# Turning a later batch's x over beside the first layer's projections, and the first batch's statistics from PSUM

## The chip, the cores and the metric

The kernel runs on one core of a Trainium2 chip. The metric is device time in microseconds of one execution. Times come from separate executions; the profile is of one more execution, recorded by the hardware profiler.

## The reference, cut to what matters

The input x has 8 batches of 32 x 32 positions with 512 channels, in fp32; N = 1024 positions. Two layers follow each other, and each adds an attention to its input:

```python
x = x + L0(_gn(x))   # 16 heads of 32: softmax(q k^T / sqrt(32)) v, then w_proj and b_proj
x = x + L1(_gn(x))   # 4 heads of 128, with relative position logits, then Wo
def _gn(v):          # 32 groups of 16 channels: mean and variance over positions and channels
    g = v.reshape(B, H, W, 32, 16)
    return (g - mean(g)) / sqrt(var(g) + 1e-5)
```

In each layer q, k and v are products of the normalised x (1024 x 512) with a 512 x 512 matrix each. Batches don't depend on each other.

## The kernel before

**Layout.** x comes as rows of channels, and the kernel wants it with channels on the partitions. Batch 0 is turned over by TensorE (`load_first`, L1163). The others are loaded in pieces by `load_blocks` (L289): four DMAs of 64 KB bring one half of one chunk of 128 channels, in blocks of 32 x 32, into a buffer with the tag "row", and a VectorE transpose of 128x512 turns the blocks over. The tag has three buffers, and the output (`put_out`, L1358) uses the same three: its transpose writes one, and four DMAs empty it.

**Statistics.** `look_at` (L304) runs bn_stats on each half (512 elements) of a chunk and, after the second, bn_aggr. `group_norm` (L320) averages over groups of 16 channels by two small transposes and six small VectorE instructions, has GpSimd raise the variance to the power -1/2 (rstd, L357), and normalises in four `tensor_scalar` instructions (L361). With `apart=True` the averaging and the normalising lie in different stages.

**Products.** Each 512 x 512 projection is made of two units, and each unit of seven products in place of eight (Strassen's scheme, Winograd's form). Four sums of quarters of x are made by VectorE (`forming`, L403); sums of quarters of the weights are made once and kept in DRAM. `seven` (L467) runs a unit over three PSUM banks, x, y and z. In order: product 0 into x, ACT copies it to p1; product 5 into y, and VectorE adds a = y + p1 (L481); product 1 into x; product 4 into y, and b = y + p1 (L489); product 6 into z, ACT copies it to p7; product 2 into y, addition c12; product 3 into z, addition c21 (L646); and c22 on GpSimd (L650). It yields after each product, so that other work can be woven in.

**The order of the work.** The kernel is written as generators. `side_by_side` (L1409) runs the first layer's attention of batch b (`attention_0`, 64 steps, each of 8 score matmuls, an exponential on ACT, 4 matmuls into acc, and an addition of 128x2048 on VectorE, L823) beside a list of other work, `rest`, in proportion to given costs. For a batch b in the middle, `rest` holds, in this order:

1. `after_0` and `after_1`: output projections of the first layer of batch b-1 and of the second layer of batch b-2 (with `put_out`);
2. `second`: the second layer's q, k and v of batch b-1, and its position logits;
3. `attention_1`: the second layer's attention of batch b-1, with `load` of batch b+1 woven in (`load_apart`, L1148, fetches the turned x from DRAM, normalises and forms sums);
4. `before_0`: the first layer's q, k and v of batch b+1.

`woven(main, side, start, gap, places)` (L1397) takes one piece of `side` wherever main's step count, less `start`, is in `places` modulo `gap`. Around this, a scheduler places each instruction in its engine's order; `tc.issue_after(...)` holds an instruction behind another in that order. [...] The weights are loaded by `Stream` (L199), seven products ahead.

**turn_ahead** (L1128) turns batch b+1 over ahead of `load_apart`, for b = 1 to 6. In each of eight steps it starts the load of the next half, transposes the present one (L1139), takes its statistics, and stores the turned half to DRAM (L1141). It ends with the averaging and rstd. It is woven around items 1 and 2 at every sixth step from the third:

```python
            if coming is not None:
                rest = [woven(chain(*rest), later(turn_ahead, b + 1, coming), 3, 6)]
```

Where this stands in the code, `rest` holds items 1 and 2; `attention_1` and `before_0` are appended later.

**load_first.** TensorE transposes batch 0 into eight PSUM banks: four of a wide tile for the first half of the positions, four others for the second. ACT copies each bank to SBUF (L1189). Then TensorE runs six matmuls with no use for their result, into the wide tile ("idle", L1193), VectorE takes the statistics of the copies chunk by chunk, and the copies are normalised and summed (`forms`). `before_first` starts with v's product 0.

Of the kernel before, what the change touches and what calls it, by code (L numbers as in the profile page):

```python
# [17 lines left out]
P = 128  # L18
# [9 lines left out]
def quick_path(  # L28
# [66 lines left out]
    def chunks(block):  # L95
        return [block[:, i, :] for i in range(CC)]
# [202 lines left out]
    def statistics(st, xT, cc, name):  # L299

        for h in range(NH):
            look_at(st, xT[cc][:, h * NB : (h + 1) * NB], cc, h, name)

    def look_at(st, half, cc, h, name):  # L304

        if "mv" not in st:
            st["mv"] = mvs[0]
            mvs.reverse()
        if h == 0:
            st["st"] = small.tile([P, NH, 6], F32, tag=f"st{name[0]}", name=f"st_{name}_{cc}", bufs=1)  # L310
        s = st["st"]
        nc.vector.bn_stats(s[:, h, :], half)
        if h < NH - 1:
            return
        nc.vector.bn_aggr(
            st["mv"][:, : 2 * CC].rearrange("p (s c) -> p c s", c=CC)[:, cc, :],
            s.rearrange("p h s -> p (h s)"),
        )

    def group_norm(st, xT, name, after=None, behind=None, out=None, apart=False):  # L320

        mv = st.pop("mv")

        def averages(out, src, tag):
            total = small.tile([P, 2], F32, tag=f"total{tag}", name=f"total{tag}_{name}")
            nc.vector.tensor_reduce(
                total, src.rearrange("p (g k) -> p g k", k=GROUP_CHANNELS), axis=AX.X, op=ALU.add
            )
            nc.vector.tensor_scalar(
                out.rearrange("p (g k) -> p g k", k=GROUP_CHANNELS),  # L330
                total.unsqueeze(2).to_broadcast([P, 2, GROUP_CHANNELS]),
                1.0 / GROUP_CHANNELS,
                None,
                op0=ALU.mult,
            )

        turned = small.tile([P, 32], F32, tag="turned", name=f"turned_{name}")

        with tc.issue_after(after().ins) if after is not None else nullcontext():
            nc.vector.transpose(turned, mv)  # L340
        avg = small.tile([P, 2, 32], F32, tag="avg", name=f"avg_{name}")
        averages(avg[:, 0, :], turned, 0)

        nc.vector.tensor_sub(turned, turned, avg[:, 0, :])
        nc.vector.tensor_mul(turned, turned, turned)
        averages(avg[:, 1, :], turned, 1)
        back = small.tile([P, 2, 32], F32, tag="back", name=f"back_{name}")
        nc.vector.transpose(back.rearrange("p a c -> p (a c)"), avg.rearrange("p a c -> p (a c)"))
        mean = back[:, 0, :CC]
        var = small.tile([P, CC], F32, tag="var", name=f"var_{name}")  # L350
        nc.vector.scalar_tensor_tensor(
            var, back[:, 0, CC : 2 * CC], GN_EPS, back[:, 1, :CC], op0=ALU.add, op1=ALU.add
        )
        if apart:
            yield 0
        rstd = small.tile([P, CC], F32, tag="rstd", name=f"rstd_{name}")
        nc.gpsimd.tensor_tensor(rstd, var, neg_half, op=ALU.pow)  # L357
        yield 0
        for cc in range(CC):
            with tc.issue_after(behind().ins) if behind is not None else nullcontext():  # L360
                nc.vector.tensor_scalar(  # L361
                    xT[cc] if out is None else out[cc],
                    xT[cc],
                    mean[:, cc : cc + 1],
                    rstd[:, cc : cc + 1],
                    op0=ALU.subtract,
                    op1=ALU.mult,
                )
            if cc % 2 or apart:
                yield 0  # L370
# [5 lines left out]
    begun = [None]  # L376
    half_done = [None]

    reader = [None]
    summed = [None]  # L380
    beside_norm = [False]

# [84 lines left out]
    def seven(fs, u, rows, sink, name, hook=None):  # L467

        product = taken(fs, u, rows)
        x = bank(f"x_{name}")
        product(x, 0, True)
        p1 = snapshot("e1", f"p1_{name}")
        nc.scalar.copy(p1, x)
        yield HC
        y = bank(f"y_{name}")
        product(y, 5, True)
        a = snapshot("es1", f"a_{name}")  # L480
        reader[0] = begun[0] = nc.vector.tensor_add(a, y, p1)  # L481
        sink.early(p1, a)
        yield HC
        product(x, 1, False)
        sink.c11(x)
        yield HC
        product(y, 4, False)
        b = snapshot("es1", f"b_{name}")
        reader[0] = half_done[0] = nc.vector.tensor_add(b, y, p1)  # L489
        sink.middle(b)  # L490
        yield HC
        z = bank(f"z_{name}")
        product(z, 6, True)
        p7 = snapshot("e1", f"p7_{name}")
        nc.scalar.copy(p7, z)  # L495
        yield HC
        product(y, 2, False)
        sink.c12(y, p1)
        if hook is not None:
            hook()  # L500
        yield HC
        product(z, 3, False)
        sink.c21(z, a)
        sink.c22(b, p7)
        yield HC

# [120 lines left out]
    class Plain:  # L627
# [15 lines left out]
            nc.vector.tensor_add(self.dst[1][0], self.shape(y), self.shape(p1))  # L643

        def c21(self, z, a):
            nc.vector.tensor_add(self.dst[0][1], self.shape(z), self.shape(a))  # L646

        def c22(self, b, p7):
            s = self.shape
# [478 lines left out]
    def turn_ahead(b, st):  # L1128

        parts = [(cc, h) for cc in range(CC) for h in range(NH)]  # L1130
        ahead = [load_blocks(b, *parts[0])]
        st["kept"] = [
            dram.tile([P, N], F32, tag="kept", name=f"d_0_{b}_{cc}", bufs=4 * CC) for cc in range(CC)
        ]
        for i, (cc, h) in enumerate(parts):
            if i + 1 < len(parts):
                ahead.append(load_blocks(b, *parts[i + 1]))
            t = mem.tile([P, NB], F32, tag="row", name=f"xt_{b}_{cc}_{h}", bufs=3)
            nc.vector.transpose(t, ahead.pop(0))  # L1139
            look_at(st, t, cc, h, f"0_{b}")  # L1140
            nc.sync.dma_start(st["kept"][cc][:, h * NB : (h + 1) * NB], t)  # L1141
            yield 0
        st["x0"] = []
        st["norm0"] = group_norm(st, st["x0"], f"0_{b}", behind=lambda: added[0], apart=True)
        for _ in range(2):
            yield next(st["norm0"])
# [16 lines left out]
    def load_first(st):  # L1163

        rows = block("x_rows", [P, NT, C])
        for t in range(NT):
            queue = nc.scalar if t % 2 else nc.sync
            queue.dma_start(rows[:, t, :], xf[0, t * P : (t + 1) * P, :])
        for m in (WV0, WQ0, WK0):
            m.fetch(nc.sync)  # L1170
        x = block("x0T_0")
        xT = chunks(x)
        for h in range(NH):
            if h == 0:
                whole = wide_tile("turned_0")
                banks = [whole[:, cc, :] for cc in range(CC)]
            else:
                banks = [bank(f"turned_1_{cc}") for cc in range(CC - 1)]
                banks.append(psum.tile([P, NB], F32, tag="acc", name="turned_1", bufs=1))
            for t in range(NT // NH):  # L1180
                for cc in range(CC):
                    nc.tensor.transpose(
                        banks[cc][:, t * P : (t + 1) * P],
                        rows[:, h * (NT // NH) + t, cc * P : (cc + 1) * P],
                        ident,
                    )
            for cc in (0, 2, 1, 3):
                part = xT[cc][:, h * NB : (h + 1) * NB]
                nc.scalar.copy(part, banks[cc])  # L1189

        idle = wide_tile("idle")
        for t in range(6):
            nc.tensor.matmul(idle[:, t % CC, :], ident, rows[:, t, :], start=True, stop=True)  # L1193
        for cc in (0, 2, 1, 3):
            statistics(st, xT, cc, "0_0")
        st["kept"] = put_away(xT, "0_0")

        xn = block("xn0_0")
        run(group_norm(st, xT, "0_0", out=chunks(xn)))
        st["xn"] = forms(xn, "xn0_0")  # L1200

# [293 lines left out]
    for b in range(B + 1):  # L1495
# [14 lines left out]
        if last is not None:  # L1510
# [21 lines left out]
                total += PRODUCT // 2  # L1532
            rest.append(later(second, b - 1, last))
            total += SECOND
            if coming is not None:
                rest = [woven(chain(*rest), later(turn_ahead, b + 1, coming), 3, 6)]
            if past is not None and coming is not None:

                total -= 1
# [27 lines left out]
        if coming is not None:  # L1567

            before = later(before_0, b + 1, coming, forms_0 if last is not None else None)
            rest.append(before if last is not None else woven(before, other_sums(), 2, 7))  # L1570
            total += 3 * PRODUCT - PRODUCT // 2
        if b == 0:
# [501 lines left out]
```

## Time and profile before

| what | value |
|---|---|
| median of 3 runs | 3688.07 us (3687.99 to 3688.77) |
| the profiled execution's own time | 3690.96 us |
| its span, first to last instruction | 3688.8 us |
| mean granted TensorE clock | 0.996 |
| transposes of turn_ahead (L1139) | 48, of 703 ns |
| their statistics (L312, xt) | 48, of 691 ns |
| attention additions (L823) | 448, of 2405 ns |
| loads of x (xs) | 224 by SP, 64 KB each, 2.7 us to landing |
| stores of turned halves (d<-xt) | 48 by SP, 256 KB each, 2.4 us |
| output pieces (out<-ot) | 240 by SP, 64 KB each, 2.0 us |

A batch in the middle takes about 448 us: the output projections 43 us each, the second layer's q, k and v 45, 41 and 44, its attention 112, and the first layer's q, k and v 44, 43 and 33. These limits are where PE changes from one product's name to the next.

How to read it. PE is TensorE's matmuls and PEld its loads of stationary operands; DVE is VectorE, ACT ScalarE, POOL GpSimd, SP SyncE, which only issues DMAs. L391 is the line in a helper that issues every projection matmul, so the tile's name tells which: y_q is bank y of a unit of q. An fp32 matmul shows as two records; "x16" are eight instructions. Matmuls of 32 columns run four at a time, so a product of 16 records of 128x512 takes 1.72 us. The profile puts the idle time of an engine down to the semaphore event that came last ("<-DVE a_q L481"); "issue" means that it shows no such event. Idle time of an engine off the path costs nothing.

### The profile page before, as it was taken

The page shows a single profiled execution, that of the slowest core. Times are in us where ns is not written, and L with a number is a line of the kernel's source. Part 1 is how long each engine was busy: PE and PEld are TensorE (multiplying, and loading weights), DVE is VectorE, ACT ScalarE, POOL GpSimd, SP SyncE. Part 2 cuts the span into 40 slices and gives each one's busy share as a digit, 9 for nine tenths or more (in the row PEclk, how much of TensorE's full clock was granted, in tenths as well). Part 3 has the DMA queues.
Part 4 walks back from the last instruction along what each step waited for, and adds up shares of the span by engine and source line. Part 5 has one row for each costly group of instructions (what it writes and reads, how often), then busy time and mean ns, then how long its engine had stood idle before and what let it go on. Part 6 is the DMA issues. An engine that isn't in the chain of part 4 may idle for free.

```text
span 3688.8 us, 81250 instructions
## 1 busy us (share of the span) xinstructions
PE 3641.0 (99%) x33992; PEld 1244.9 (34%) x33998; DVE 2547.7 (69%) x2905; ACT 1999.0 (54%) x2281; POOL 1288.6 (35%) x833
## 2 busy tenths in 40 slices
PE   8999999999999999999999999999999999999998
PEld 4222244232442224332343323433234332333343
DVE  6878757678565876658666696666957678567546
ACT  2555566545664466544665446654466545656254
POOL 1342146121451316413163131721318112165254
PEclk9999999999999999999999999999999999999999
DMA  6223255144641346423463245623436233325386
GB/s 190 75 75 110 75 153 155 38 124 107 166 143 61 108 103 186 124 92 80 114 192 104 95 93 126 190 77 101 110 99 195 58 100 78 99 90 156 95 202 145
DMA packets 582071, 432.00 MB, mean 117 GB/s; under 512 B 280608, under 2 KB 472384, under 8 KB 580672
## 3 DMA queue, kind: packets, MB, share of 16 engines
q1 hardware_dynamic: 570064, 410.92, 40.3%
q0 software_dynamic: 2608, 13.70, 1.0%
q8 instruction: 270, 4.42, 0.5%
q10 hardware_dynamic: 9024, 2.10, 0.3%
q14 instruction: 105, 0.86, 0.1%
HBM read 334.30 MB, written 92.27 MB: 116 GB/s over the span
## 4 chain that ended last, share of the span: by engine, by line
PE 94%; DVE 3%; DMA 1%; issue 1%; ACT 1%; POOL 0%; SPq 0%; ACTq 0%; DVEq 0%; POOLq 0%
PE ps L785 14%; PE acc L811 13%; PE ps L1004 12%; PE acc L1018 12%; PE y_v L391 5%; PE y_k L391 4%; PE y_q L391 4%; PE x_v L391 3%; PE z_v L391 3%; PE x_k L391 3%; PE z_k L391 3%; PE z_q L391 3%; PE x_q L391 3%; PE y_wp L391 2%; PE y_wo L391 2%; PE sums L833 2%
## 5 line engine op out<-in xcount | busy, mean ns | idle before, releaser
L800 ACT ACTIVATE e_room<-ps 128x2048 f32<-128x2048 f32 x512 | 961.9, 1879 | 763.6 <-PE ps L785 739.8
L823 DVE TENSOR_TENSOR e_room<-e_room 128x2048 f32<-128x2048 f32 x448 | 1077.3, 2405 | 413.7 <-ACT e_room L800 412.4
L954 POOL TENSOR_TENSOR pos<-pos,columns 128x512 f32<-128x512 f32 x448 | 642.7, 1452 | 193.0 <-DMA pos<-pr 190.4
L785 PE MATMUL ps<-q,k 32*64 32x512 f32 x8192 | 593.4, 613 | 1.0 <-ACT e_room L800 1.0
L811 PE MATMUL acc<-e_room,v 128*32 128x512 f32 x4096 | 546.8, 604 | 0.1
L1004 PE MATMUL ps<-q,k 128*128 128x512 f32 x1024 | 530.2, 600 | 0.5 <-ACT ps L963 0.5
L1018 PE MATMUL acc<-e,v 128*128 128x512 f32 x1024 | 523.0, 593 | 0.0
L1007 ACT ACTIVATE e<-ps 128x512 f32<-128x512 f32 x512 | 305.8, 597 | 323.9 <-PE ps L1004 315.0
L1034 DVE TENSOR_TENSOR es<-es,e 128x512 f32<-128x512 f32 x384 | 277.7, 723 | 214.2 <-ACT e L1007 210.8
L1018 PEld LDWEIGHTS acc<-e,v 128*128 128x128 f32 x1024 | 193.3, 190 | 247.6 <-issue 133.0
L963 ACT COPY ps<-pos 128x512 f32<-128x512 f32 x448 | 264.7, 592 | 10.4 <-PE ps L976 7.5
L766 POOL TENSOR_TENSOR q<-q,su 128x512 f32<-128x512 f32 x64 | 105.0, 1640 | 461.5 <-DVE su L762 450.4
L1004 PEld LDWEIGHTS ps<-q,k 128*128 128x128 f32 x1024 | 187.3, 190 | 231.0 <-issue 207.2
L785 PEld LDWEIGHTS ps<-q,k 32*64 32x64 f32 x8192 | 123.0, 130 | 391.9 <-issue 215.0
L811 PEld LDWEIGHTS acc<-e_room,v 128*32 128x32 f32 x4096 | 81.4, 108 | 412.3 <-issue 365.2
L650 POOL TENSOR_TENSOR k<-b_k,p_k 128x512 f32<-128x512 f32 x32 | 48.5, 1515 | 483.5 <-ACT p_k L495 483.5
L650 POOL TENSOR_TENSOR q<-b_q,p_q 128x512 f32<-128x512 f32 x32 | 61.7, 1929 | 363.7 <-ACT p_q L495 268.2
L650 POOL TENSOR_TENSOR v<-b_v,p_v 128x512 f32<-128x512 f32 x32 | 55.5, 1735 | 352.5 <-ACT p_v L495 349.6
L883 ACT COPY pos<-pp 32x512 f32<-32x512 f32 x128 | 104.5, 816 | 29.2 <-PE pp L874 27.9
L1032 DVE TENSOR_TENSOR es<-e,e 128x512 f32<-128x512 f32 x64 | 64.0, 1000 | 72.5 <-ACT e L1007 72.5
L391 PE MATMUL y_q<-f_xn,w_q 128*32 128x512 f32 x768 | 93.6, 606 | 14.7 <-DVE f_xn L430 9.3
L727 DVE STREAM_TRANSPOSE tu<-su 128x512 f32<-128x512 f32 x64 | 45.2, 706 | 85.8 <-ACT su L725 85.7
(229 smaller groups left out, 4562.7 us busy)
## 6 DMA issues: line engine op xcount, KB each, us to landing
pos<-pr SPq DMA_DIRECT2D x448, 256.0 KB, 3.5
w_qkv<-ws_qkv SPq DMA_DIRECT2D x168, 128.0 KB, 2.6
x1T<-d SPq DMA_DIRECT2D x32, 512.0 KB, 5.6
d<-x1T SPq DMA_DIRECT2D x32, 512.0 KB, 3.6
pc<-pos SPq DMA_DIRECT2D x32, 512.0 KB, 6.5
pr<-pos SPq DMA_DIRECT2D x32, 512.0 KB, 7.7
columns<-pc SPq DMA_DIRECT2D x64, 256.0 KB, 4.3
x2T<-d SPq DMA_DIRECT2D x32, 512.0 KB, 6.7
```

What stands on the lines that cost most here:

```text
L391: ins = nc.tensor.matmul(out[columns, :], weights[:, columns], moving, start=start, stop=stop, skip_group_check=open_sum,)
L650: nc.gpsimd.tensor_tensor(self.dst[1][1], s(b), s(p7), op=ALU.add)
L785: nc.tensor.matmul(ps[some, r, :], k[m][rows, j * P + 64 * i : j * P + 64 * i + 64], q[m][rows, h * NB : (h + 1) * NB], start=True, stop=True,
L800: exps[0] = nc.scalar.activation(e, ps, AF.Exp, scale=D0 ** -0.5)
L811: nc.tensor.matmul(acc[r * D0 : (r + 1) * D0, :], v[:, j, c0 : c0 + D0], e[:, r, :], start=(j == blocks[0]), stop=(j == blocks[-1]),)
L823: summed[0] = nc.vector.tensor_add(state["esum"], state["esum"], e)
L954: nc.gpsimd.tensor_tensor(self.rows[i], self.rows[i], self.columns[i // NT], op=ALU.add)
L963: self.copied = nc.scalar.copy(ps, rows)
L1004: scored[0] = nc.tensor.matmul(ps, k[h][:, keys], q[:, h, queries], start=False, stop=True, skip_group_check=True)
L1007: exps[0] = nc.scalar.activation(e, ps, AF.Exp, scale=1.0 / math.sqrt(D1))
L1018: nc.tensor.matmul(acc, v[:, j, h * D1 : (h + 1) * D1], e, start=(j == 0), stop=(j == NT - 1),)
L1034: added[0] = nc.vector.tensor_add(state["esum"], state["esum"], e)
```

## The change

**1. Batch 0's statistics.** Each bn_stats reads the PSUM bank, right behind ACT's copy of it, into a buffer of its own ("looks"); the four bn_aggr come together afterwards. The two chains, copies and statistics, are held in the order of the program. There are eight idle matmuls in place of six.

**2. turn_ahead.** It is no longer woven around items 1 and 2 of the list. It is woven around `before_0` of batch b+1, for batch b+2 (b = 0 to 5), so a batch is turned over one round earlier than before. Its pieces come after every seventh product and the fourth behind it; each transpose is issued behind the last addition, c21, of the unit at hand (for the first half of a chunk) or behind its addition b (for the second).

**3. What this needs.** The mean is copied out of the averaging's buffer, since the normalising comes a stage later, and it and rstd get buffers of their own in that case. The small statistics buffer is shared by both layers. `c21` hands its instruction back. The function `aggregate` is the second half of `look_at`, unchanged.

TensorE's order is that of before, except in the first few products of batch 0.

```diff
@@ group_norm
         if apart:
+
+            mean = small.tile([P, CC], F32, tag="mean0", name=f"mean_{name}")
+            nc.vector.tensor_copy(mean, back[:, 0, :CC])
             yield 0
-        rstd = small.tile([P, CC], F32, tag="rstd", name=f"rstd_{name}")
+        rstd = small.tile([P, CC], F32, tag="rstd0" if apart else "rstd", name=f"rstd_{name}")
@@ seven
-        sink.c21(z, a)
+        closed[0] = sink.c21(z, a) or closed[0]
@@ turn_ahead
-            nc.vector.transpose(t, ahead.pop(0))
+            with tc.issue_after((closed if h == 0 else half_done)[0].ins):
+                nc.vector.transpose(t, ahead.pop(0))
             look_at(st, t, cc, h, f"0_{b}")
@@ load_first
+        looks = mem.tile([P, NB], F32, tag="row", name="looks", bufs=3)
+        looks = looks[:, : CC * NH * 6].rearrange("p (c h s) -> p c h s", c=CC, s=6)
+        looks = [looks[:, cc] for cc in range(CC)]
+        looked, copied = [None], [None]
...
-                nc.scalar.copy(part, banks[cc])
+                with tc.issue_after(copied[0].ins) if copied[0] is not None else nullcontext():
+                    copied[0] = nc.scalar.copy(part, banks[cc])
+                with tc.issue_after(looked[0].ins) if looked[0] is not None else nullcontext():
+                    looked[0] = nc.vector.bn_stats(looks[cc][:, h, :], banks[cc])
 
         idle = wide_tile("idle")
-        for t in range(6):
+        for t in range(NT):
             nc.tensor.matmul(idle[:, t % CC, :], ident, rows[:, t, :], start=True, stop=True)
+        st["mv"] = mvs[0]
+        mvs.reverse()
         for cc in (0, 2, 1, 3):
-            statistics(st, xT, cc, "0_0")
+            aggregate(st, looks[cc], cc)
@@ the list of work
-            if coming is not None:
-                rest = [woven(chain(*rest), later(turn_ahead, b + 1, coming), 3, 6)]
...
             before = later(before_0, b + 1, coming, forms_0 if last is not None else None)
+            if b + 2 < B:
+                n = len(ORDER)
+                before = woven(before, later(turn_ahead, b + 2, states[b + 2]), n - 1, n, (0, 4))
```

More of the change, by code (lines that the diff above doesn't have):

```diff
@@ L309, in look_at @@
         if h == 0:
-            st["st"] = small.tile([P, NH, 6], F32, tag=f"st{name[0]}", name=f"st_{name}_{cc}", bufs=1)
+            st["st"] = small.tile([P, NH, 6], F32, tag="st", name=f"st_{name}_{cc}", bufs=1)
         s = st["st"]
@@ L314, in look_at, with aggregate @@
             return
+        aggregate(st, s, cc)
+    def aggregate(st, s, cc):
         nc.vector.bn_aggr(
@@ L377, in quick_path @@
     half_done = [None]
-    reader = [None]
+    reader, closed = [None], [None]
     summed = [None]
@@ L645, in c21 @@
         def c21(self, z, a):
-            nc.vector.tensor_add(self.dst[0][1], self.shape(z), self.shape(a))
+            return nc.vector.tensor_add(self.dst[0][1], self.shape(z), self.shape(a))
         def c22(self, b, p7):
```

## The prediction

> **What bounds the kernel now.** I read the page first: how busy each engine is, and what the chain of work that ended last is made of.
>
> ```profile
> PE 3641.0 (99%) x33992; PEld 1244.9 (34%) x33998; DVE 2547.7 (69%) x2905; ACT 1999.0 (54%) x2281; POOL 1288.6 (35%) x833
> ...
> PE 94%; DVE 3%; DMA 1%; issue 1%; ACT 1%; POOL 0%; SPq 0%; ACTq 0%; DVEq 0%; POOLq 0%
> ```
>
> TensorE sets the time. No matmul of the layers is removed, so the change can only win back time in which PE stands still or runs slowly, or add such time: 3688.8 - 3641.0 = 47.8 us of span are all there is. So I went through PE's timeline and looked for every matmul with idle time before it. In each line: start, duration, work, and in brackets the idle time and what ended it.
>
> ```profile
> 11.39 5.32 PE L1193 MATMUL idle<-x_rows,ident 128*128 128x512 f32 x12
> 21.71 3.64 PE L391 MATMUL x_v<-prep_qkv,xn 128*32 128x256 f32 x32 [5.01 <-issue]
> ...
> 104.43 1.06 PE L833 MATMUL sums<-e_room,ones 128*32 128x512 f32 x8 [1.70 <-DVE e_room L823]
> ...
> 371.07 2.60 PE L391 MATMUL y_k<-f_xn,w_qkv 128*32 128x512 f32 x16 [2.44 <-DVE a_k L481]
> ...
> 399.83 3.42 PE L391 MATMUL y_q<-f_xn,w_q 128*32 128x512 f32 x16 [4.76 <-DVE a_q L481]
> ...
> 866.08 2.67 PE L391 MATMUL y_q<-f_xn,w_q 128*32 128x512 f32 x16 [2.93 <-DVE f_xn L430]
> ```
>
> The last of these comes back at the same place in each later batch, shorter: 1.63 us at 1315, 1.43 at 1763, 1.88 at 2211, 1.44 at 2659. It is always the second layer's first projection, waiting for DVE. Batch 7, at 3108, has only 0.63 us there; at that point no batch is left to turn over. The chain of waits at 1315 shows what DVE was late with:
>
> ```profile
> 1305.85 0.63 DVE ot L1364
> ...
> 1307.94 1.98 DMA out<-ot
> ...
> 1310.04 0.72 DVE xt L1139
> ...
> 1310.78 2.35 DMA d<-xt
> ...
> 1313.59 0.68 DVE b_q L489
> 1314.27 1.14 DVE f_xn L430
> ...
> 1315.46 1.92 PE y_q L391 x16
> ```
>
> DVE works in order. The turning over of the next batch's x (L1139) waits for one of the three buffers that it shares with the output, then its second transpose for its own store, and the sums that PE needs (b_q, f_xn) stand behind. Last, how full DVE is there and where the turning over goes to (each row: stretch, length, then PE, PEld, DVE, ACT, POOL busy us):
>
> ```profile
> 1092.40:1136.00 43.60, 43.60 (x454) 11.26 (x457) 27.41 (x28) 22.07 (x18) 4.50 (x3) 1.00 0.14 41
> 1136.00:1179.20 43.20, 43.20 (x452) 11.03 (x448) 25.89 (x22) 21.48 (x17) 4.50 (x3) 1.00 0.15 44
> 1179.20:1212.40 33.20, 33.20 (x556) 16.35 (x549) 20.48 (x21) 10.32 (x11) 5.00 (x3) 1.00 0.53 180
> 1298.90:1344.00 45.10, 43.47 (x452) 10.85 (x448) 39.42 (x50) 25.47 (x22) 10.30 (x5) 1.00 0.64 141
> ```
>
> The first three rows are the first layer's q, k and v: DVE is 60 to 63% busy and PE never idle. The fourth is the second layer's q: DVE 39.42 of 45.10, or 87%.
>
> **What the Trainium skill says.** "TensorE: Matmul & The Clock Gate", section "What's actually happening": PE runs at half its clock after an idle window of about 3.4 us, and until it has been busy for about as long. The trace agrees in kind, not in the figure: after 5.01, 4.76 and 2.93 us of idle, and already after 2.44, matmuls take double (16 in 2.60 to 3.42 us in place of 1.72); after 1.88 and less they don't. "PSUM — Partial Sum Buffer", section "PSUM bank collisions raise a hardware error": two engines may not read one bank at once, so software must order them. No row of before shows it, but the built order of the new program does: each statistics instruction waits for ACT's copy of the same bank. "DMA: Bandwidth & Descriptors", "Anatomy of one DMA", gives about 2 us fixed for a transfer (on the software path); here, on the hardware path, a turned half is stored in 2.4 us and an output piece lands in 2.0.
>
> **The change part by part.** *First batch's statistics from PSUM.* Before, the eight statistics wait for all copies of a chunk and end, with the last aggregate, at 17.59. Now they follow ACT's copies bank by bank. ACT's first copy ends near 9.25; the trace has two statistics in 1.29 us, 0.645 each from SBUF. No row has one from PSUM: an add from PSUM takes 0.69 and one from SBUF 0.69, so I take the same, with 0.60 to 0.75 as ends (0.4 us either way over eight, plus 0.8). Four end at 11.9, eight at 14.5, four aggregates of 0.21 to 0.24 at 15.5: 2.1 us earlier. The chain from there to the first matmul (4.05 us, from 17.63 to 21.68) is unchanged, so that comes at 19.6. The idle matmuls wait until four statistics have left the wide tile (11.9 in place of 11.4) and now number 8, 16 records of 0.43: they end near 18.9, and the gap falls from 5.0 to 0.7 us. So PE should start at full clock. But the built order puts y_v right behind x_v, and y_v needs two sums from DVE that end 5.5 us after the normalising starts (20.80 to 26.30 before): at 24.2. A new gap of about 2.6 us, perhaps a slow stretch after it. From there DVE rules: the normalised sums end at 26.5, five weight sums (0.62 each) at 29.6, a_v at 30.3, three more products of 1.72 and the rest of the sums carry v to about 36.9, where before q took PE over at 40.3. **3.6 us gained**; 1.0 if PE is slow throughout, 5.5 if nothing waits.
>
> *Turning over, at its old place.* Per batch 8 transposes (703 ns by the groups by shape) and 8 statistics (691), 4 aggregates of 0.21, the averaging chain of 2.0 us: 8 x 1.39 + 0.84 + 2.0 = 14.0 us of DVE, for six batches. What goes of the stalls: at 371, DVE works without a break from 361, and two transposes with their statistics, 2.7 us, leave it: the 2.44 go, and the slow 0.88 + 0.90 (y_k 2.60 and ps 1.94 for 1.72 and 1.04) with them: 4.2. At 400, five such pairs and the chain, about 8 us, stand ahead of a_q: 4.76 + 1.70 = 6.5. At 866: 2.93 + 2 x 0.95 = 4.8. Then 1.6, 1.4, 1.9, 1.4. Sum 21.8. At 1315 I checked what is late next: without the pair, a_q ends near 1305.8, two additions of 2.2 us follow, b_q at 1310.9, f_xn at 1312.1; PE comes to it at 1313.8. So the stall goes with 1.7 us to spare, and I leave 0.2 us a batch for the rest (batch 7's is 0.63): 1.4. **20.4 us gained.** The built order of before also had three transposes of batch 2 between 92.8 and 102, ahead of the addition that PE waits for at 104.43: **1.7 us** more.
>
> *At its new place.* In the first layer's projections, one pair behind a unit's last addition (c21) or behind b. Nothing in it feeds PE soon; queued behind it are an attention addition (2.2 to 2.4 us), and the additions that free a PSUM bank. Cover: by the timelines of DVE and PE, in batches 2 and up the last attention addition ends 2.5 to 3.7 us before PE's sums want it, and a bank is wanted two products (3.4 us) after its addition could start. A pair is 1.39, so it fits. It doesn't where the averaging chain lies behind the last pair (1.39 + 0.2 + 2.0 + 0.1 = 3.7 us together) nor always in batch 0, where DVE is 42.2 of 53.0 us busy and the cover before the sums is 1.5 to 2.2. SP's queue gets 4 loads and a store (about 2.4 us of issuing) for each pair, between weight loads that run seven products ahead: hidden unless DVE stands still for some 7 x 1.72 = 12 us. POOL's power for rstd (2.0 us) moves with it; behind it waits v's addition (L650), wanted much later. The added copy of the mean, 128x4, is one instruction like var's 0.16, six times. I take 0.5 us a batch: **3 us lost**; ends 0 and 10.
>
> Sum: 3.6 + 20.4 + 1.7 - 3.0 = 22.7 us. The profiled execution took 3690.96 us (span 3688.8 and 2.2 around it): 3690.96 - 22.7 = 3668.3. Against the median of the runs, 3688.07: **3665.4**.
>
> **The rivals.** *The stalls only shrink* (25%): the output's transposes share buffers with L1139 but wait for their own transfers too, and DVE at 87% less 14.0 of 45 us still holds late additions; batch 7 with 0.63 and 0.37 us of idle speaks for it, my check at 1315 against. Half of 20.4 is lost: 22.7 - 10.2 = 12.5 gained, 3675.6. *Moved, not removed* (7%): the pairs stall the first layer's projections about as much as they did the second's; 17 to 25 us come back, within 0.2% (7.4 us) of before, which is about what a measurement can tell: near 3687. *Slower* (5%): in the new place each pair lies on PE's path through the additions behind it. All of it would be 6 x 14.0 = 84 us; the gain of 25.7 is used up from 31% on, and at half, 42 us, the time is 3688 - 26 + 42 = 3704. DVE's 37% of idle time there and the cover above speak against. *The start does more* (3%): with PE at full clock and no new gap, 30 us, 3658.
>
> **How the numbers follow.** The forecast has 60%, 3660 to 3670. Leaving out the rivals on the far sides and one end of each unknown cost, 8 in 10 lie between 3658 and 3676. Faster by over 0.2%: 60 + 25 + 3 = 88%; within: 7%; slower: 5%.
>
> **What would show it.** Right: no idle time over 0.5 us ahead of y_q in the second layer's first projection; no transposes xt there; DVE at 70 to 75% in the first layer's projections with PE still without gaps; the first x_v near 19.6, and q from about 37. Wrong: gaps ahead of sums or y in the first layer's projections; y_q still behind the output's transposes; or w_qkv loads landing late behind SP's loads of x.

## The result, and the profile after

| | before | after |
|---|---|---|
| median of the runs | 3688.42 us (3686.26 to 3691.14, 6 runs) | 3663.98 us (3663.53 to 3664.69, 6 runs) |
| profiled execution, span | 3690.96, 3688.8 us | 3663.89, 3662.1 us |

The ratio is 0.9933, 95% interval 0.992 to 0.9946: 24.4 us less. The forecast was 3665.4, the range 3658 to 3676. The runs of after lie within 1.2 us, those of before spread over 4.9; experiment 5 comes back to that.

The page of after, the engines' busy time and the chain of work:

```profile
PE 3633.3 (99%) x33996; PEld 1243.4 (34%) x34002; DVE 2557.9 (70%) x2911; ACT 1999.3 (55%) x2281; POOL 1298.3 (35%) x833
...
PE 95%; DVE 3%; ACT 1%; issue 1%; POOL 0%; DMA 0%; SPq 0%; DVEq 0%; ACTq 0%; POOLq 0%
```

PE's busy time fell by 7.7 us though it has four records more: matmuls ran less often at half their speed (the mean granted clock is 0.999 in place of 0.996). Span without a busy PE fell from 47.8 to 28.8 us. So of the 26.7 us between the two spans 19.0 are standing time and 7.7 slow time. DMA's share of the chain went from 1% to 0%.

Where the second layer's first projection stood still in batches 2 to 6, PE's timeline now has no bracket, in batch 3 for instance (the place of 1315.46 before):

```profile
1295.13 1.90 PE L397 MATMUL y_q<-f_xn,w_q 128*32 128x512 f32 x16
1296.84 1.90 PE L397 MATMUL z_q<-x1T,w_q 128*32 128x512 f32 x16
```

DVE's timeline at that place shows why: no transpose of x stands between a_q and f_xn, and nothing waits for a transfer (over the whole kernel DVE's waits for DMAs went from 8.1 us to none). DVE even has idle time, in which it waits for ACT's exponentials:

```profile
1287.13 0.67 DVE L487 TENSOR_TENSOR a_q<-y_q,p_q 128x512 f32<-128x512 f32 x1
1287.73 2.27 DVE L829 TENSOR_TENSOR e_room<-e_room 128x2048 f32<-128x2048 f32 x1
1290.86 2.29 DVE L829 TENSOR_TENSOR e_room<-e_room 128x2048 f32<-128x2048 f32 x1 [0.86 <-ACT e_room L806]
1293.07 0.68 DVE L495 TENSOR_TENSOR b_q<-y_q,p_q 128x512 f32<-128x512 f32 x1
1293.67 1.22 DVE L436 TENSOR_TENSOR f_xn<-x1T,f_xn 128x1024 f32<-128x1024 f32 x1
```

f_xn ends at 1294.89, a quarter of a microsecond before PE comes to it. The stretches again (first layer's q, k, v; second layer's q; columns as before):

```profile
1073.80:1117.50 43.70, 43.70 (x455) 11.31 (x458) 30.15 (x33) 22.07 (x18) 4.51 (x3) 1.00 0.25 65
1117.50:1160.70 43.20, 43.20 (x452) 11.01 (x448) 31.56 (x32) 21.48 (x17) 4.51 (x3) 1.00 0.38 93
1160.70:1193.90 33.20, 33.20 (x560) 16.38 (x552) 24.96 (x36) 10.32 (x11) 7.38 (x4) 1.00 0.57 198
1280.40:1323.70 43.30, 43.30 (x455) 10.96 (x451) 31.00 (x27) 25.51 (x22) 8.25 (x4) 1.00 0.34 73
```

In the first layer's projections DVE is now 69, 73 and 75% busy, and PE still fills each stretch. The second layer's q takes 43.30 us in place of 45.10, with DVE at 72% in place of 87%. The slack in the new place shows in the same trace: in before, an attention addition at 1116.14 waits 0.86 us for ACT; in after, a pair of transpose and statistics (1096.67) stands ahead of the same addition, which then follows at 1098.02 without a wait. Batch 7 keeps its 0.63 us, and one other gap of that kind is left, at batch 1:

```profile
387.30 1.92 PE L397 MATMUL y_q<-f_xn,w_q 128*32 128x512 f32 x16 [0.65 <-DVE a_q L487]
```

**The ledger.** How far after is ahead of before when PE takes up each piece, from the two profiled executions:

| up to | lead, us | gained in this piece | forecast |
|---|---|---|---|
| first layer's q of batch 0 takes PE over | 2.7 | 2.7 | 3.6 |
| past the sums at 104 | 4.6 | 1.9 | 1.7 |
| batches 0 and 1 in the new place, to the stall at 371 | 4.4 | -0.2 | part of -3.0 |
| past 371 | 8.4 | 4.0 | 4.2 |
| past 400 | 14.1 | 5.6 | 6.5 |
| new place again, to 866 | 13.7 | -0.4 | part of -3.0 |
| past 866 | 18.5 | 4.8 | 4.8 |
| past 1315, 1763, 2211, 2659 | 26.1 | 1.8, 1.6, 2.4, 1.7 | 1.6, 1.4, 1.9, 1.4 |
| end (gained behind the last matmuls) | 26.7 | 0.6 | |

The start, with idle time in brackets:

```profile
13.92 8.53 PE L1207 MATMUL idle<-x_rows,ident 128*128 128x512 f32 x16 [2.96 <-DVE looks L1203]
22.39 1.93 PE L397 MATMUL x_v<-prep_qkv,xn 128*32 128x256 f32 x32
25.35 1.93 PE L397 MATMUL y_v<-prep_qkv,f_xn 128*32 128x256 f32 x32 [1.03 <-DVE f_xn L436]
...
37.63 1.91 PE L397 MATMUL x_q<-xn,prep_qkv 128*32 128x512 f32 x16
```

This isn't the start I forecast: the idle matmuls begin at 13.92, not 11.9, and the first x_v comes at 22.39, later than before. They also took 8.53 us for 16 records in place of 16 x 0.43 = 6.9: part of them ran slowly after the gap of 2.96 us.

### The profile page after: what moved, and what is told of

Read it like the earlier page. It is cut to its first block, busy times and chain, and to the rows that moved or that the text cites. A ratio compares the mean times of both kernels' runs of the same rounds, so it can differ in the third digit from the quotient of the medians.

```text
span 3662.1 us, 81197 instructions
## 1 busy us (share of the span) xinstructions
PE 3633.3 (99%) x33996; PEld 1243.4 (34%) x34002; DVE 2557.9 (70%) x2911; ACT 1999.3 (55%) x2281; POOL 1298.3 (35%) x833
## 4 chain that ended last, share of the span: by engine, by line
PE 95%; DVE 3%; ACT 1%; issue 1%; POOL 0%; DMA 0%; SPq 0%; DVEq 0%; ACTq 0%; POOLq 0%
PE ps L791 15%; PE acc L817 13%; PE ps L1010 12%; PE acc L1024 12%; PE y_v L397 4%; PE y_q L397 4%; PE y_k L397 4%; PE z_q L397 3%; PE x_v L397 3%; PE z_v L397 3%; PE x_k L397 3%; PE x_q L397 3%; PE z_k L397 3%; PE y_wp L397 2%; PE y_wo L397 2%; PE sums L839 2%
```

## Experiments

My theory: nearly all of the gain comes from the old place, where the pairs of transpose and statistics stood behind transfers and ahead of sums that PE wanted, and the new place has slack for them. The rivals: the start is worth several microseconds of its own; the pairs cost something at the new place too; it is DVE's amount of work, not its waits, that stalled PE at the old place.

**1 and 2. Each part alone.** start_only takes only load_first from the change, move_only leaves only it out.

The main lines of the edits, the second in words:

```diff
@@ start_only, against after
-                before = woven(before, later(turn_ahead, b + 2, states[b + 2]), n - 1, n, (0, 4))
+                rest = [woven(chain(*rest), later(turn_ahead, b + 1, coming), 3, 6)]
@@ move_only, against after
-    load_first of after
+    load_first of before
```

> The kernel before with the change of the first batch's statistics alone (PSUM, eight idle matmuls). If the two parts are independent, the traces say what this one is worth: q's first product ends 2.7 us earlier in the changed kernel (its copy starts at 39.60 in place of 42.26), so 2.7 us less than before, some 3685.7, with the stalls at 371, 400, 866 and so on as before. Rival: the lead is used up at the first place where DVE is late (the sums at 104), then under 1 us is left, 3687.5 or more.

> The changed kernel with the first batch's statistics and idle matmuls as before: the moved turning over alone. If the parts are independent: the whole gain of the medians, 24.4 us, less 2.7, is 21.7, so 3666.7; the x_v of the start at 21.7 again with a slow stretch. Rival: the stalls go because everything of batch 0 and 1 runs earlier; then several of them (104, 371, 400) come back and the gain is under 15 us, 3673 or more.

start_only: 3691.72 us (3687.18 to 3696.9, 13 runs), ratio 1.0004, interval 0.9996 to 1.0013. move_only: 3664.25 (3662.56 to 3665.13, 5 runs), ratio 0.9932, 0.9918 to 0.9945. So the move alone gives the whole gain, and the start alone none that can be measured. The 2.7 us that the traces had shown for the start, on which the expected 3685.7 and 3666.7 stood, are in neither.

**3 and 4. The two once more, on one chip.** after_again is after, move_again is move_only.

> The kernel after once more, beside the next on one chip, so that the statistics part alone can be told from their difference: 3663.5 to 3664.7.

> The kernel after with the old start (the turning over moved, the statistics taken from the copies as before, six idle matmuls), beside the kernel after on one chip. If the start's lead that the traces show (q takes over 1.5 us later here than in after) reaches the end: 1.2 to 1.8 us more than after. If not: within 0.5 us of it.

after_again: 3663.97 us (3663.75 to 3664.97, 5 runs). move_again: 3663.14 (3662.86 to 3663.27, 5 runs). The statistics part isn't worth 3.6 us; here the kernel without it is 0.8 us faster, which neither expectation had. The old start is not the same in each execution. PE's timeline in move_only:

```profile
20.94 3.64 PE L397 MATMUL x_v<-prep_qkv,xn 128*32 128x256 f32 x32 [4.88 <-issue]
25.28 3.19 PE L397 MATMUL x_v<-prep_qkv,xn 128*32 128x256 f32 x25 [0.69 <-ACT p_v L482]
```

and the same two groups in move_again:

```profile
21.44 3.22 PE L397 MATMUL x_v<-prep_qkv,xn 128*32 128x256 f32 x32 [5.01 <-issue]
25.36 1.70 PE L397 MATMUL x_v<-prep_qkv,xn 128*32 128x256 f32 x25 [0.70 <-ACT p_v L482]
```

The second group takes 3.19 us in one execution and 1.70 in the other: the slow stretch after the gap ends late or early. q takes PE over at 39.3 and at 37.6. The new start gave 37.6 to 37.9 in after, after_again, after_idle6 and double, so in these traces it saves 0 to 2.7 us, mostly by how long the slow stretch of the old one lasts. The 0.8 us the other way are not wholly explained: 0.25 of them show at q, and 0.35 at the gap ahead of y_q in batch 1, which is 0.30 in move_again and 0.65 in after_again.

**5. A better start with the old turning over.** start_free is start_only with the four banks of free_banks (experiment 8).

> The kernel before with the first batch's statistics from PSUM in four tiles of one bank each, the turning over at its old place: the best start (about 4.5 us ahead of before when q takes over) with the old stalls behind it. If a lead adds up as it does with the turning over at its new place: before less 4 to 5, about 3685. If the stalls behind it change with each execution and swallow it, as with the start alone (3691.7 where 3685.7 was expected): 3688 to 3693, with a spread of 5 us or more.

3688.07 us (3685.37 to 3691.76, 13 runs), ratio 1.0, 0.9991 to 1.0008: the second expectation. Its trace shows where the lead goes: 5.2 us when q takes over, still 4.9 when the second layer's q of batch 4 begins at 1741.7, and 1.3 when its k begins. One place takes 3.6 us. The DVE line and the PE line there in start_free:

```profile
1754.64 0.71 DVE L1142 STREAM_TRANSPOSE xt<-xs 128x512 f32<-128x512 f32 x1 [2.78 <-DMA out<-ot]
...
1760.05 2.79 PE L394 MATMUL y_q<-f_xn,w_q 128*32 128x512 f32 x12 [3.43 <-DVE f_xn L433]
```

and in before:

```profile
1757.52 0.71 DVE L1139 STREAM_TRANSPOSE xt<-xs 128x512 f32<-128x512 f32 x1 [0.79 <-DMA out<-ot]
...
1762.94 1.92 PE L391 MATMUL y_q<-f_xn,w_q 128*32 128x512 f32 x16 [1.43 <-DVE f_xn L430]
```

The same transpose waits 2.78 us for the output's transfer in one and 0.79 in the other; PE stands 3.43 us in place of 1.43 and then runs slowly, 3.52 us for the 16 records of y_q in place of 1.92. So of the 3.6 us, 2.0 are the longer wait and 1.6 the slow stretch behind it. The program of this stretch is the same in both. DVE takes its work in order here: PE had written the bank that b_q reads by 1752.87, DVE stood idle until 1754.64, and b_q still ran behind the waiting transpose, at 1758.18.

The traces of the three kernels with an earlier start and the old turning over (start_only, before_idle12, start_free) all have the long wait at this place, 2.49 to 2.78 us; before, without the lead, has the short one. Whether the lead itself brings the long wait about, or it differs from one execution to the next, can't be told apart, since only one execution of each was profiled. So two causes are likely for the spread of before's runs, and neither is measured: such waits, and slow stretches that differ too (y_q in batch 5 took 3.30 us behind a gap of 1.91 in start_only, and 1.92 behind 1.88 in before). A lead won at the start is kept in free_banks (experiment 8), where DVE waits for no transfer; here it was lost at one such wait.

**6. Freeing the shared buffers.** out_in_place is before with the output's transposes in place, so that the three buffers are left to x.

```diff
-            ot = mem.tile([P, NB], F32, tag="row", name=f"ot_{b}_{m}_{h}", bufs=3)
+            ot = xT[m][:, h * NB : (h + 1) * NB]
```

> The kernel before, with the turning over at its old place, but the output's transposes write in place, into the chunk that they read, so that they no longer use the three buffers of the turning over. Theory that waiting for a shared buffer makes DVE late: from batch 2 on the stalls ahead of y_q (4.8, 1.6, 1.4, 1.9, 1.4 us with their slow stretches, 11.1 together) go almost wholly, those of batch 1 (371 and 400, 10.7 us, where no output is written yet) stay: 8 to 11 us less than before, about 3678. Theory that the work itself makes DVE late: under 3 us less, 3685 or more.

3714.99 us (3713.78 to 3716.92, 5 runs), ratio 1.0072, 1.0058 to 1.0086: neither. The second layer's q lost its stalls from batch 2 on (at most 0.40 us is left), as the theory of waits wants it; one pair still stands between a_q and b_q there (at 1317.28 in batch 3), but doesn't wait. But in batch 3 three pairs then came earlier, in the output projection, where before has one, and stood behind the other transfer, the store of the half before. DVE and PE in that trace:

```profile
1263.67 0.71 DVE L1139 STREAM_TRANSPOSE xt<-xs 128x512 f32<-128x512 f32 x1 [2.69 <-DMA d<-xt]
```

```profile
1286.69 3.59 PE L391 MATMUL y_wo<-f_ao,w_o 128*32 128x512 f32 x16 [3.81 <-DVE x2T L666]
```

Two waits for d<-xt took 4.0 us in this batch, the 2.69 ahead of the output projection's additions and 1.33 later, and the output projection took 50 us in place of 43. One wait was removed, and a longer one with three pairs of work behind it took its place. How much of it is the wait and how much the work wasn't separated. The transposes in place may add to it.

**7. Work without transfers at the old place.** work_only is after with statistics of a resident tile added there.

```diff
+    def look_twice(st, b):
+        for i in range(CC * NH):
+            s = small.tile([P, NH, 6], F32, tag="st", name=f"st_again_{b}_{i}", bufs=1)
+            for h in range(NH):
+                nc.vector.bn_stats(s[:, h, :], st["v"][:, i, :])
+            yield 0
...
+                rest = [woven(chain(*rest), look_twice(here, b), 3, 6)]
```

> The kernel after, and at the turning over's old place (items 1 and 2 of the list, every sixth step from the third, b = 1 to 6) two more statistics instructions a step over a resident 128x512 of the first layer's v, into a buffer that nobody reads: 16 x 0.69 = 11.0 us of VectorE work a batch where the turning over had 8 x 1.39 + 0.84 + 2.0 = 14.0, with no shared buffer and no DMA to wait for. If what stalled TensorE there was VectorE's waits for transfers (the output's piece and the turned half leaving the shared buffers), the stalls stay away: 3664 to 3667. If it was the amount of work (VectorE at 87% in that stretch), most of the 20 us of stalls come back: 3675 to 3684.

3698.44 us (3698.34 to 3700.48, 9 runs), ratio 1.0027, 1.0017 to 1.0037: 34.5 us more than after for 66 us of work, outside both expectations. But the work didn't lie where the pairs had lain. It ran in a lump behind the second layer's own statistics, probably because they use the same single small buffer. DVE, and PE behind it:

```profile
1251.96 5.25 DVE L1159 BATCH_NORM_STATS2 st_again<-v 128x6 f32<-128x512 f32 x8
```

```profile
1257.86 1.92 PE L397 MATMUL y_wo<-f_ao,w_o 128*32 128x512 f32 x16 [2.31 <-DVE a_wo L487]
```

From batch 2 on, the stalls are in the output projection, none ahead of y_q. The run doesn't decide between work and waits for the second layer's q. It does say that work alone stalls PE in these items too: behind lumps of 5 us in the output projection, and in batch 1 by 3.92 us ahead of y_k (368.14).

**Work or waits in the trace of before.** The trace of before itself tells them apart in part. Ahead of the stall at 400, DVE waits for no transfer: the view of its waits from 357 to 400 us lists only one, 1.0 us for PE. It works without a break, with pieces of the turning over between the others, and a_q, for which PE stands 4.76 us, comes last:

```profile
390.46 0.70 DVE L1139 STREAM_TRANSPOSE xt<-xs 128x512 f32<-128x512 f32 x1
...
396.30 0.70 DVE L1139 STREAM_TRANSPOSE xt<-xs 128x512 f32<-128x512 f32 x1
396.92 2.25 DVE L823 TENSOR_TENSOR e_room<-e_room 128x2048 f32<-128x2048 f32 x1
399.09 0.68 DVE L481 TENSOR_TENSOR a_q<-y_q,p_q 128x512 f32<-128x512 f32 x1
```

So the stalls at 371 and 400 come from the amount of work, and so does the one at 104, with three pairs and no wait for a transfer ahead of it. Together they are 11.5 of the ledger's 23.9 us. From batch 2 on, one transpose between a_q and f_xn waits for out<-ot, 2.28 us in batch 2 and 0.79 or 0.80 in the others: 5.5 us in all, where PE stands 9.3 us. Behind each wait DVE is busy up to f_xn, so the waits count in full; the rest is the work of the pairs. The theory that it is the waits holds for over half of the standing time from batch 2 on, and for none of it ahead of that.

**8. The first half's banks apart.** In after, ACT's copies and DVE's statistics take turns. ACT's timeline:

```profile
8.41 0.59 ACT L1201 COPY x0T<-turned 128x512 f32<-128x512 f32 x1 [4.47 <-PE turned L1193]
9.76 0.59 ACT L1201 COPY x0T<-turned 128x512 f32<-128x512 f32 x1 [0.77 <-DVE looks L1203]
```

The second copy, of another bank, waits for the statistics of the first: 1.35 us a bank, where ACT alone took 2.06 us for four in before. Both banks belong to one tile. free_banks makes four tiles of them.

```diff
-                whole = wide_tile("turned_0")
-                banks = [whole[:, cc, :] for cc in range(CC)]
+                close_wide()
+                four = tc.tile_pool(name="four", bufs=1, space=PSUM)
+                four = (four, four.__enter__())
+                banks = [
+                    four[1].tile([P, NB], F32, tag=f"t{cc}", name=f"turned_0_{cc}", bufs=1)
+                    for cc in range(CC)
+                ]
```

> The kernel after, with the first half of batch 0 turned over into four tiles of one bank each in place of one tile of four banks, so that a copy of one bank and the statistics of another need not follow each other. If the tile is what made them alternate, the eight statistics end about 1.5 us earlier and the idle matmuls begin earlier too. If a lead at the start reaches the end of the kernel, 1 to 2 us less than after: 3662 to 3663. If it doesn't (with the old start the new place of the turning over gave 3664.25), within 0.7 us of after: 3663.3 to 3664.7.

3661.58 us (3661.46 to 3661.87, 5 runs), ratio 0.9919, 0.9905 to 0.9932: 2.4 us less than after, and the fastest of all. DVE, then PE:

```profile
8.49 2.49 DVE L1208 BATCH_NORM_STATS2 looks<-turned 128x6 f32<-128x512 f32 x4 [4.97 <-ACT x0T L1206]
```

```profile
11.04 7.13 PE L1214 MATMUL idle<-x_rows,ident 128*128 128x512 f32 x16 [0.17 <-DVE looks L1208]
18.58 2.18 PE L397 MATMUL x_v<-prep_qkv,xn 128*32 128x256 f32 x32 [0.41 <-issue]
```

Four statistics now take 2.49 us together, x_v comes at 18.58, q at 35.5 in place of 37.6. That lead of 2.2 us is 2.4 at the end: in this kernel a lead stays.

**9 and 10. The number of idle matmuls.** after_idle6 has six in place of eight; before_idle12 is before with twelve in place of six.

```diff
@@ after_idle6
-        for t in range(NT):
+        for t in range(6):
@@ before_idle12
-        for t in range(6):
+        for t in range(12):
...
```

> The kernel after, with six idle matmuls in place of eight at the start. In the profile of after the eight ended at 22.39, 1.8 us after the normalised x was there, so TensorE reached the first product late. If that delay is on the path: the first product starts 1 to 2 us earlier, and 0 to 1.5 us come off, 3662.5 to 3664. If the sums that the next product waits for set the pace, the gap behind the first product grows by as much as it starts earlier, and the time stays within 0.5 us, or grows by up to 2 us if TensorE's clock falls after the gap: 3663.5 to 3666.

> The kernel before with twelve idle matmuls in place of six, which last until about 21.7, when the first x_v can start; nothing else. Theory that the clock makes a good part of the start's gain: the first products run at full clock (some 20 rounds of four matmuls, 0.21 us less each, of which about half is then spent waiting for DVE's sums), 1.5 to 3 us less than before, about 3686. Theory that DVE alone sets the start: within 0.7 us of before.

after_idle6: 3664.41 us (3663.75 to 3664.56, 5 runs), as after. x_v comes at 20.89, 1.5 us earlier, but the gap ahead of y_v grows from 1.03 to 2.54, and y_v starts at 25.36 where after has 25.35. So the sums on DVE set the pace there, as the prediction had it, and not the idle matmuls. before_idle12: 3692.77 (3690.29 to 3697.08, 21 runs), ratio 1.0009, 1.0002 to 1.0015: about 3 us more than before, outside both expectations. In its trace x_v runs at nearly full speed (2.11 us in place of 3.64), and q takes over 2.0 us earlier; at the end nothing of that is left. As in start_free, the transpose ahead of y_q in batch 4 waits 2.69 us for out<-ot.

**11 and 12. More of the work at the new place.** double does each transpose and each statistics instruction twice, fourfold four times.

```diff
-                nc.vector.transpose(t, ahead.pop(0))
+                xs = ahead.pop(0)
+                for _ in range(1 + 1):
+                    nc.vector.transpose(t, xs)
             look_at(st, t, cc, h, f"0_{b}")
+            for _ in range(1):
+                nc.vector.bn_stats(xs[:, :6], t)
```

> The kernel after, with each of the 48 transposes at the new place done twice into the same tile, and each of the statistics done twice (the second into a buffer that is read no more): 48 x 1.39 = 67 us more of VectorE work in the first layer's projections, and the buffer of the loaded half comes free 1.4 us later. Cover theory: a pair of 1.39 us lies in 2.5 to 3.7 us of slack, so two pairs (2.8 us) still fit nearly everywhere; at most 0.2 us for each, under 10 us in all and likely 0 to 3: 3664 to 3667 us. Path theory (each pair stands ahead of additions that TensorE waits for, and part of its own cost is in the kernel after already): half or more of 67 us, 3697 or more.

> The kernel after, with each transpose and each statistics instruction at the new place done four times: 3 x 67 = 200 us more of VectorE work there. Cover theory with the slack of 2.5 to 3.7 us that the profile of before showed: 5.6 us for each in place of 1.4 is 1.9 to 3.1 us past the slack, for 48 of them 90 to 150 us more than after, 3755 to 3815 us, with gaps ahead of sums and y in the first layer's projections. If the slack is larger than I read it (a late addition is made up for by the next), under 30 us more. Path theory: near 200 us more, 3864.

double: 3666.91 us (3666.31 to 3667.9, 5 runs), ratio 0.9933, 0.992 to 0.9947: 2.9 us more than after for 67 us of work, 4%. fourfold: 3735.26 (3733.93 to 3737.36, 4 runs), ratio 1.0118, 1.0102 to 1.0133: 71 us more for 200, 36%. The first is what slack says and the path theory excludes; the second is less than the 90 to 150 I worked out, since in the last four of the six batches the stalls gather in two places (about 4.2 us each, with slow matmuls behind). In fourfold's PE timeline:

```profile
1150.60 1.94 PE L397 MATMUL y_k<-f_xn,w_qkv 128*32 128x512 f32 x8 [4.20 <-DVE a_k L487]
```

In double two gaps are new, 1.01 us at 273.64 and 1.38 at 736.45, both at attention steps: there the limit begins to show.

## Why the prediction was right, and which terms were not

**What bounds it, and the stalls at the old place: right.** The ledger has 23.9 us for the seven stalls and the one at 104, where 21.8 + 1.7 were forecast. Each is within 1.0 us of its forecast. The working for 1315 held: y_q starts without a gap, though f_xn is 0.25 us early and not 1.7; DVE now waits 0.86 us for ACT's exponentials, and a_q comes some 0.7 us later against PE than I had it. The mechanism, a transpose that waits for the output's transfer with the sums queued behind it, shows most plainly in batch 4 (0.79 and 2.78 us of wait, 1.43 and 3.43 of stall). One reading was wrong: "then its second transpose for its own store". In DVE's timeline of batch 3 that transpose runs at 1315.32, behind f_xn; ahead of b_q and f_xn stand one pair and an attention addition. At 400, four transposes and three statistics stood ahead of a_q since the stall before, not five pairs. And 47.8 us were not all there was to win: a slow matmul counts as busy, and 7.7 us of PE's busy time went too.

**"I leave 0.2 us a batch for the rest: 1.4": too much.** 0.65 us at 387 are left, nothing in batches 2 to 6, and batch 7's 0.63 as before. The rival "the stalls only shrink" fell with that.

**"I take 0.5 us a batch: 3 us lost": too much.** The ledger shows 0.2 and 0.4 us in all. double prices a second load of the same work at 2.9 us, so the first, which fits the slack of 2.5 to 3.7 us, should cost less. Of the rivals, "moved, not removed" and "slower" needed 17 to 42 us here.

**"3.6 us gained" at the start: the step that failed.** Two things in it. First, "they follow ACT's copies bank by bank": the next copy also waits for the statistics of another bank of the same tile, so the aggregates ended at 16.50, not 15.5, the idle matmuls began 2.0 us late and ran 1.6 us longer than 16 x 0.43, and x_v came at 22.39, not 19.6. (The price of the statistics from PSUM was right: in free_banks four take 2.49 us, and the aggregates end at 14.01.) Second, I took the slow stretch of the old start (x_v 3.64 and 3.19 us) as what that start costs; in another execution of the same start (move_again) the second group ran at full speed. The trace's 2.7 us were that execution's, and side by side the part gave -0.8. What I had right is that y_v's sums rule: six and eight idle matmuls give the same y_v.

So the sum came out 1.4 us from the median partly by luck. The start was forecast at 3.6 us and gave 0.3 (after against move_only, from different sets of runs) or -0.8 (after_again beside move_again). The move was forecast at 20.4 + 1.7 - 3.0 = 19.1 us and gave 25.4 (move_only) and 25.7 (move_again) against before: the new place costs nearly nothing, little is left of the stalls, and some of the rest lies in the time of before that it is taken from. The two errors have opposite signs. The forecast stands on one profiled execution of before, and before's medians lay between 3688.1 and 3691.4 us in different sets of runs.

**Still open:** how large y_q's stalls from batch 2 on would be with the work or the waits alone at the old place. Experiments 6 and 7 each moved the pairs or the work elsewhere, and no kernel was run in which the turning over has buffers of its own there.

## What to carry to other kernels

Before moving work off an engine's queue, ask what the moved instruction waits for, and count its work and its wait apart: here a pair was 1.4 us of work, and in five of the batches one transpose waited a further 0.8 to 2.8 us for a transfer, with PE's operands behind both. Look for a stretch where the engine has idle time between deadlines, and test the slack by doing the work twice: 4% of its price says that it is hidden, and the next doubling (36% here) says where that ends. A lead won early counts only if no later wait is set by something that doesn't move with it; and a difference in one profiled execution that lies in a slow stretch should be seen twice before it is put in a sum.

## What the runs showed of the hardware

**Slow matmuls behind a gap.** No single length of gap decides it in these runs. After 1.91 us (start_only, 2215.55) the 16 records of y_q took 3.30 us, at a mean granted clock of 0.56; after 3.17 us (out_in_place, 369.85) those of y_k took 1.92, at 1.00. The idle matmuls of one kernel ran at 0.53 for their first 3.1 us after a gap of 2.96 us (after) and at 1.00 throughout after 3.57 (after_again). In work_only PE stood 2.31 or 2.32 us at the same place of five batches: once y_wo then took 3.43 us at 0.54 (1709.54), four times 1.92 at 1.00. Nor is the return fixed. After gaps of 4.88 us in move_only and 5.01 in move_again, which are one kernel, the first group ran at 0.50 and 0.59, the second at 0.50 and 1.00.

The Trainium skill ("TensorE: Matmul & The Clock Gate", section "What's actually happening") has PE slow down after an idle window of about 3.4 us, and says that this window runs freely, whenever a kernel starts, so that the number of slow matmuls differs from run to run. The variation agrees with these runs; slow matmuls after 1.91, 2.31 and 2.44 us (y_k at 371 in before, at 0.71 over its 2.6 us) don't agree with a whole idle window of 3.4.

**Banks of one PSUM tile.** ACT and DVE, which read different banks of one tile, took turns in after at 1.35 us a bank; with tiles of one bank each, four statistics ran in 2.49 us beside the copies. This is how the program that was built ordered them; it isn't a limit of the banks, since the same reads ran together in free_banks.
